# Expert outputs added in memory by accumulating DMAs, with the routing weights gathered beside the token rows

## The chip, the core and the metric

The kernel runs on one core of a Trainium2 chip. A core has a matrix engine (TensorE, PE in the profile; its weight loads are PEld), a vector engine (VectorE, DVE), a scalar engine (ScalarE, ACT), a general engine (GpSimd, POOL) and a sequencer that issues DMAs (SyncE, SP). Each engine takes its instructions in order, and they meet through semaphores. On-chip memory is SBUF (128 partitions) and PSUM (128 partitions, banks that matrix products are written to); inputs, outputs and scratch tensors are in HBM, reached by 16 DMA engines. Plain DMAs are issued here by SyncE. Indirect DMAs, which take a row number for each of 128 partitions, are issued by GpSimd.

The metric is the device time of one execution in microseconds (us). The kernel before took 928.88 us, the median of three runs (928.79 to 930.76).

## The reference, cut to what matters

Six layers work on x of 64 x 32 = 2048 tokens with 256 features; each adds its result to x. Two attention layers, an fp8 linear layer, a cross attention with a context of 257 keys and a gated low-rank mixer come first. The change is in the last layer, a mixture of experts on the normalized tokens:

```python
flat = hidden.reshape(T, d)                              # 2048 x 256
router_probs = softmax(flat @ router_w + router_b)       # 8 experts
topk_probs, topk_idx = top_k(router_probs, 2)
weights = zeros_like(router_probs).at[arange(T)[:, None], topk_idx].add(topk_probs)
sh = gelu(flat @ sw1 + sb1, approximate=False)           # the shared expert
shared_out = sh @ sw2 + sb2
h1 = gelu(einsum('td,edh->teh', flat, rw1) + rb1[None], approximate=False)
expert_out = einsum('teh,ehd->ted', h1, rw2) + rb2[None]
mixed = einsum('ted,te->td', expert_out, weights)
return shared_out + mixed                                # added to x
```

Each token needs only its two chosen experts. The hidden width is 512, and all of this is in float32.

## The kernel before

**Tokens.** x stays in SBUF as four groups `xs[g]` of 128 x 4 x 256: partition p of tile t in group g is token g*512 + t*128 + p. At the start of the last layer the normalized rows `y` are stored in the HBM tensor `y_rows` (2048 rows of 256 numbers) and, transposed, kept in SBUF for the router and the shared expert. The helper `normed` does this for some tiles of a group; `choose` turns router products into the probabilities `pe` and two one-hot choices `best`.

**Routing.** `mixture` sorts the 4096 pairs of token and expert into tiles that belong to one expert each. There are 16 places for wide tiles (256 rows, `n` = 2, numbers j = 0 to 15) and further narrow ones (128 rows, `n` = 1, j from 16 on). `MS` = 20 tiles are always computed, 16 wide and 4 narrow; up to 3 more are in a branch (`tc.If(count > MS)`), which these inputs do not take. VectorE works out the place of each pair (`pos`) and the probability of each choice (`pw`, by `picked`). Then it writes one-hot matrices `in_tile` and `at`, and TensorE multiplies them in four batches into `ps_inv`, which holds for each place of each tile the row number of its pair: 1 to 2048 for a first choice, 2049 to 4096 for a second one, 0 for none. From it come `read_i` (which row of `y_rows` to gather) and `write_i` (which row to write the result to; a spare row where the place is empty).

**The expert loop.** For tile j: `gather(j)` fetches rows of `y_rows` into `yg`, one indirect DMA for each 128 rows; `first_weights` and `second_weights` load w1, w2 and the bias b2 of the tile's expert (514, 512 and 128 KB); `by_feature` transposes the rows on TensorE (`ps_yg`); `hidden` computes `ps_h` on TensorE and gelu on ScalarE; `outputs` computes `ps_o` on TensorE, adds b2 on VectorE (`og`) and scatters the rows by one indirect DMA for each 128 rows into the HBM tensor `r_rows`, which has a row for each pair. The scatters are declared independent of one another. The loop is written out by hand: iteration j gathers tile j+3, transposes tile j+1, computes the hidden layer of j and the outputs of j-1. Buffers come from rings of three or four tiles.

**The shared expert.** Its hidden layer is computed in 16 pieces (`fill_hidden`), its output in 16 units (`fill_outputs`), one for each 128 tokens: four matrix products into half a PSUM bank, `ps_so`. After two units VectorE owes an addition of the full bank to x (`owed`, paid by `settle`). Seven units are placed by hand within the routing, three before the loop, six after it.

**The end.** After the last tile SyncE loads all of `r_rows` back (8 DMAs `r<-r_rows` of 512 KB), and `sum_up` adds to x the two expert rows of each token, each times its `pw`, in 32 VectorE instructions, and stores x to `out`.

Names in the profile: L106 is the line of a helper that issues nearly all instructions of VectorE, ScalarE, GpSimd and SyncE; L118 and L121 are matrix products and transposes. So groups are told apart by their tiles. A scheduler settles the final order of each engine's instructions, where the kernel does not ask for program order.

Of the kernel before, what the change touches and what calls it, by code (L numbers as in the profile page):

```python
# [7 lines left out]
F32 = mybir.dt.float32  # L8
# [56 lines left out]
def perceiver_kernel(ctx: ExitStack, tc: tile.TileContext, a: dict, out: bass.AP):  # L65
# [810 lines left out]
    def normed(g, ts, eng=None, by_act=True):  # L876

        n, t0 = len(ts), ts[0]
        x = xs[g]
        steps = norm_steps(g, eng, True, ts, by_act)  # L880
        next(steps)
        yield
        next(steps)
        yield
        if n > 2:
            next(steps)
            yield
        y = finish(steps)
        sync.dma_start(
            out=y_rows.rearrange("(g t p) d -> g p t d", g=NG, p=P)[g][:, t0 : t0 + n], in_=y  # L890
        )
# [58 lines left out]

    hid_bank, out_bank = either("b3", "b4"), ring(psum, "b2", "b6")
    hidden_rows = {}
# [13 lines left out]
    def shared_outputs(g, t):  # L966
        if t % 2 == 0:
            out_rows[0] = out_bank([P, 2, D], "ps_so")
# [12 lines left out]

    out_rows = [None]
    owed = []

    def settle():
# [11 lines left out]
    def fill_outputs(n):  # L997
        for _ in range(n):
            shared_outputs(*next(output_units))
# [482 lines left out]
    def mixture():  # L1482
        nt = nt_all
        n2 = 2 * nt

        r_rows = nc.dram_tensor("r_rows", (2 * NB * S + MH * P, D), F32, kind="Internal").ap()
        pm = ring(psum, "b5", "b7")
# [3 lines left out]
        def carved(tag, shape, name, dt=F32, size=256):  # L1491
# [13 lines left out]
            return part  # L1505

        rc = sb.tile([P, N_ROUTE], F32, tag="n0", name="rc")
        sync.dma_start(out=rc, in_=a["route"])
# [33 lines left out]
        fill_outputs(1)  # L1542
        next(last_norm)
        next(last_norm)
        next(early, None)
# [27 lines left out]
        fill_hidden(7)  # L1573
        pos, pw = carved("w8", [n2], "pos"), carved("w8", [n2], "pw")

        def picked(which, dst, src):
            pick = carved(("f4", "lx0")[which], [nt, NE], "pick")
            vector.tensor_tensor(pick, best[which], src, ALU.mult)
            vector.tensor_reduce(dst[:, which * nt : (which + 1) * nt], pick, AX.X, ALU.add)

        for which in range(2):
            picked(which, pw, pe)

# [46 lines left out]
        for which in range(2):  # L1630
            picked(which, pos, place)
        pos_i = carved("lx3", [n2], "pos_i", I32)
# [30 lines left out]
        b2_ = ring(sb, "lx0", "lx1", "lx2")  # L1663
        yg_, ygT_ = ring(sb, "n1", "p0", "p1", "sc0"), ring(sb, "sc1", "eT0")
        hTr_, og_ = ring(sb, "q0", "q1"), ring(sb, "e0", "e1", "e2", "eT1")

# [5 lines left out]
        def gather(j):  # L1672
            n, at = its[j]["n"], its[j]["at"]
            its[j]["yg"] = yg = yg_([P, n, D], "yg")
# [30 lines left out]

        for j in range(3):
            first_weights(j)
# [62 lines left out]
        write_i = carved("lv1", [MH], "write_i", I32)  # L1770
        vector.scalar_tensor_tensor(write_i, row1, -1.0, spare, ALU.add, ALU.add)

        def by_feature(it):
# [24 lines left out]

        written = []

        def outputs(it):
            n, hT, w2, b2 = it["n"], it["hT"], it["w2"], it["b2"]
            ps = po([P, n, D], "ps_o")
            for i in range(n):
                for c in range(4):
# [6 lines left out]
                    )  # L1812
            o = og_([P, n, D], "og")
            vector.tensor_tensor(o, ps, b2[:, None, :].to_broadcast([P, n, D]), ALU.add)
            for i in range(n):
                at = it["at"] + i
                wrote = nc.gpsimd.indirect_dma_start(  # L1817
                    out=r_rows,
                    out_offset=bass.IndirectOffsetOnAxis(ap=write_i[:, at : at + 1], axis=0),
                    in_=o[:, i, :],  # L1820
                    in_offset=None,
                )
                for earlier in written:
                    tc.declare_no_dep(wrote.ins, earlier, reason="no two places have one row")
                tc.keep_in_program_order(wrote)
                written.append(wrote.ins)

        for j in range(3):
            gather(j)
        for j in range(2):  # L1830
            second_weights(j)

        count = nc.values_load(
# [19 lines left out]
        settle()  # L1853
        by_feature(its[0])
        for j in range(MS):
            if j + 3 < MS:
                gather(j + 3)
            if j + 1 < MS:
                by_feature(its[j + 1])
            hidden(its[j])  # L1860
            if j + 3 < MS:
                first_weights(j + 3)
            if j > 0:
                outputs(its[j - 1])
            if j + 2 < MS:
                second_weights(j + 2)
        outputs(its[MS - 1])


        r_view = r_rows[: 2 * NB * S].rearrange("(w g t p) d -> g p w t d", w=2, g=NG, p=P)  # L1870
        whole = sb.tile([P, 4, NT, D], F32, tag="kb0", name="r")
        r = [(whole[:, 0], whole[:, 1]), (whole[:, 2], whole[:, 3])]
        r_ = ring(sb, *wide[0:4])
        r += [tuple(r_([P, NT, D], "r") for _ in range(2)) for _ in range(2)]
        for g in range(NG):
            for which in range(2):
                sync.dma_start(out=r[g][which], in_=r_view[g, :, which])

        def sum_up(g):
            for t in range(NT):  # L1880
                x = xs[g][:, t, :]
                for which in range(2):
                    at = which * nt + g * NT + t
                    vector.scalar_tensor_tensor(
                        x, r[g][which][:, t, :], pw[:, at : at + 1], x, ALU.mult, ALU.add
                    )
                if t % 2 == 1:
                    sync.dma_start(out=out_view[g][:, t - 1 : t + 1], in_=xs[g][:, t - 1 : t + 1])

        fill_outputs(4)  # L1890
        settle()
        sum_up(0)
        fill_outputs(2)
        settle()
        for g in range(1, NG):
            sum_up(g)

    out_view = out.rearrange("(g t p) d -> g p t d", g=NG, p=P)
    mixture()
# [33 lines left out]
def _routing():  # L1933
# [10 lines left out]
    c[:, T_COL : T_COL + MT] = [2 * j if j < MF else MF + j for j in range(MT)]  # L1944
    c[:, T_SPARE : T_SPARE + MH] = 2 * NB * S + 1 + np.arange(MH) * P + p[:, None]
    return c
# [107 lines left out]
```

## Time and profile before

| | us |
|---|---|
| median of three runs | 928.88 |
| the profiled execution | 928.56 |
| its span, first to last instruction | 926.8 |
| PE busy | 856.0 |
| PEld busy | 588.5 |
| DVE busy | 605.3 |
| POOL busy | 501.1 |
| ACT busy | 424.1 |
| start of the last layer's routing table load (rc) | 697.6 |
| first gather of expert rows | 759.2 |
| first ps_h of the expert loop | 768.0 |
| last og written | 900.3 |
| last store to out issued | 923.6 |

The busy times are shares of the whole span, of which the first 700 us are attention. The last layer is read from the instructions' order in time: up to 759 us the routing, to 768 the first gathers, to 900 the expert loop, then the end. The page also cuts the span into 40 slices of 23.2 us and prints the busy share of each in tenths (9 is 90% or more); the last nine digits of each row, from 718 us on, are the routing, the expert loop and the end. PEclk is the TensorE clock that was granted, in tenths of full speed; DMA is the mean busy share of the 16 DMA engines:

```profile
PE   6899999979899999999999999999889889999993
DVE  7888888897677677675777666878654872111116
PEclk9999999989999999999999999999799979999997
DMA  7445333543110111111110112000001046777758
```

### The profile page before, as it was taken

What the parts mean: (1) busy time and instruction counts of PE and PEld (TensorE: products, weight loads), DVE (VectorE), ACT (ScalarE), POOL (GpSimd) and SP (SyncE); (2) the same over time, 40 slices, a digit from 0 to 9 for tenths busy, and PEclk for the clock granted to TensorE, in tenths of its full rate; (3) what the DMA queues carried; (4) which work ended last, traced back from release to release, by engine and by line L of the source; (5) the groups of instructions that cost most, each with busy time, mean ns of one, the idle gap of its engine ahead of it and who ended that gap; (6) DMA issues with size and microseconds to landing.
All of it is one profiled execution on the core that took longest, in us unless ns stands there. A gap on an engine that the chain in (4) does not pass through costs nothing. (4 is left out here: it accounts for less than half of the span.)

```text
span 926.8 us, 22828 instructions
## 1 busy us (share of the span) xinstructions
PE 856.0 (92%) x8699; PEld 588.5 (63%) x8699; DVE 605.3 (65%) x1755; ACT 424.1 (46%) x1099; POOL 501.1 (54%) x982
## 2 busy tenths in 40 slices
PE   6899999979899999999999999999889889999993
PEld 3566666656456666666656666565656648888882
DVE  7888888897677677675777666878654872111116
ACT  2566666645555555554555456564443212222210
POOL 3567667764674656564664747656531214555430
PEclk9999999989999999999999999999799979999997
DMA  7445333543110111111110112000001046777758
GB/s 240 140 133 141 85 88 101 132 115 104 53 52 8 46 53 53 52 54 52 53 52 3 52 52 98 2 2 24 2 23 35 24 143 189 235 240 229 216 182 272
DMA packets 66926, 88.79 MB, mean 96 GB/s; under 512 B 32480, under 2 KB 50688, under 8 KB 64768
## 3 DMA queue, kind: packets, MB, share of 16 engines
q1 hardware_dynamic: 63264, 77.75, 27.6%
q0 software_dynamic: 3456, 9.44, 3.1%
q8 instruction: 69, 1.13, 0.5%
q14 instruction: 41, 0.34, 0.1%
q10 hardware_dynamic: 96, 0.13, 0.1%
HBM read 65.80 MB, written 13.11 MB: 85 GB/s over the span
## 5 line engine op out<-in xcount | busy, mean ns | idle before, releaser
L106 ACT ACTIVATE e<-e,xnm 128x257 f32<-128x257 f32 x256 | 127.2, 498 | 51.5 <-DVE xnm L106 45.5
L106 DVE CUSTOM_DVE_ANT_0 e<-ps_s,mask 128x257 f32<-128x257 f32 x256 | 93.5, 421 | 49.6 <-PE ps_s L118 47.9
L118 PE MATMUL ps_k<-ct,w_w_l1x 128*128 128x512 f32 x256 | 122.3, 600 | 1.6 <-ACT yT L106 0.6
L106 POOL TENSOR_SCALAR e<-e,xsm 128x256 f32<-128x256 f32 x256 | 121.8, 496 | 0.0
L118 PE MATMUL ps_v<-w_w_l1x,ct 128*128 128x256 f32 x512 | 121.8, 381 | 0.0
L121 PE MATMUL ps_t<-cst,e 128*128 128x128 f32 x640 | 102.9, 284 | 7.8 <-DVE eT L106 6.9
L106 DVE COPY eT<-ps_t 128x512 f32<-128x512 f32 x128 | 88.0, 687 | 30.3 <-PE ps_t L121 30.1
L118 PEld LDWEIGHTS ps_v<-w_w_l1x,ct 128*128 128x128 f32 x512 | 93.9, 191 | 11.0 <-issue 0.2
L106 POOL TENSOR_TENSOR x<-x,rows 128x256 f32<-128x256 f32 x96 | 71.3, 759 | 46.2 <-ACT y L106 19.4
L106 ACT ACTIVATE kT<-ps_k,vec 128x512 f32<-128x512 f32 x64 | 44.1, 689 | 100.5 <-PE ps_k L118 100.3
L121 PEld LDWEIGHTS ps_t<-cst,e 128*128 128x128 f32 x640 | 72.1, 142 | 26.4 <-DVE eT L106 7.8
L106 ACT ACTIVATE hTr<-ps_h,w 128x256 f32<-128x256 f32 (+1 forms) x80 | 31.4, 450 | 115.0 <-issue 82.7
L106 DVE TENSOR_TENSOR og<-ps_o,b 128x512 f32<-128x512 f32 (+1 forms) x20 | 12.8, 638 | 105.6 <-PE ps_o L118 105.6
L118 PEld LDWEIGHTS ps_k<-ct,w_w_l1x 128*128 128x128 f32 x256 | 44.5, 190 | 41.3 <-issue 35.3
L1817 POOL DMA_INDIRECT r_rows<-og,lv x36 | 35.6, 989 | 60.9 <-DVE og L106 56.0
L118 PE MATMUL ps_h<-ygT,w 128*128 128x256 f32 (+1 forms) x320 | 65.8, 359 | 0.6 <-issue 0.6
L118 PE MATMUL ps_o<-w,hTr 128*128 128x256 f32 x288 | 65.3, 379 | 0.0
L106 ACT COPY v<-ps_v 128x512 f32<-128x512 f32 x80 | 46.4, 582 | 39.5 <-PE ps_v L118 39.4
L106 POOL TENSOR_TENSOR last<-e,xsm 128x4 f32<-128x4 f32 x64 | 13.0, 204 | 88.4 <-DVE xsm L106 88.0
L118 PEld LDWEIGHTS ps_h<-ygT,w 128*128 128x128 f32 x320 | 54.9, 190 | 6.6 <-issue 0.8
L118 PEld LDWEIGHTS ps_o<-w,hTr 128*128 128x128 f32 x288 | 54.4, 190 | 7.2
L106 ACT ACTIVATE kb<-kT,cst 128x256 f32<-128x256 f32 x96 | 45.4, 512 | 26.7 <-POOL kT L106 25.1
(210 smaller groups left out, 1677.2 us busy)
## 6 DMA issues: line engine op xcount, KB each, us to landing
ct<-in_ctxT SPq DMA_DIRECT2D x16, 1024.0 KB, 5.4
w<-in_ew SPq DMA_DIRECT2D x20, 514.0 KB, 3.6
w<-in_ew SPq DMA_DIRECT2D x20, 512.0 KB, 3.7
far<-part SPq DMA_DIRECT2D x126, 64.0 KB, 2.3
v_rows<-v SPq DMA_DIRECT2D x16, 256.0 KB, 2.3
vb<-v_rows SPq DMA_DIRECT2D x64, 64.0 KB, 2.1
r<-r_rows SPq DMA_DIRECT2D x8, 512.0 KB, 8.2
b<-in_eb SPq DMA_DIRECT2D x20, 128.0 KB, 3.8
```

The costliest lines, as they stand in the source:

```text
L106: ins = getattr(self.engine, name)(*args, **kw)
L118: return kept(nc.tensor.matmul(ps, **args))
L121: return kept(nc.tensor.transpose(ps, src, eye))
L1817: wrote = nc.gpsimd.indirect_dma_start(out=r_rows, out_offset=bass.IndirectOffsetOnAxis(ap=write_i[:, at : at + 1], axis=0), in_=o[:, i, : ...
```

## The change

It touches the last layer alone.

- `y_rows` gets 258 columns. The two probabilities of each token (`pw`, now with the two choices side by side) are stored into the last two by one DMA, 16 x 128 pieces of 8 bytes, and come with the rows in each gather (`yg` has 258 columns).
- `by_feature` picks for each row the probability that belongs to the pair (`mine` tells first from second choice) into `it["share"]`, by two small VectorE instructions.
- `outputs` scales: for each 128 rows ScalarE writes `b2w` = b2 * share, and VectorE `og` = ps_o * share + b2w.
- The scatter goes into `out` itself and adds there (`compute_op=ALU.add`). Only the scatters of one tile are declared independent of each other; between tiles the dependency on `out` stays. Empty places write to 256 spare rows behind the 2048 of `out`, which are cut off on the host and filled once from a constant tile.
- x with the shared expert's output is stored to `out` as soon as each pair of units is added (`stored`). All 16 units of the shared output stand before the loop: eight in the first part of the routing, two before the ps_inv batches, one between the second and the third batch, two before the branch and three after it. They use five PSUM banks in a new order.
- The tiles are taken in the order `line`: 0, 16, 1, 2, 17, 3, 4, 18, 5, 6, 19, 7, ... 15, so that narrow tiles stand between wide ones.
- `r_rows`, its loads, the 32 additions and the stores behind them are gone.

```diff
-    y_rows = nc.dram_tensor("y_rows", (NB * S, D), F32, kind="Internal").ap()
+    y_rows = nc.dram_tensor("y_rows", (NB * S, D + 2), F32, kind="Internal").ap()
...
-            owed.append(lambda: vector.tensor_tensor(x, ps, x, ALU.add))
+
+            def stored():
+                vector.tensor_tensor(x, ps, x, ALU.add)
+                sync.dma_start(out=out_view[g][:, t - 1 : t + 1], in_=x)
+
+            owed.append(stored)
...
+        out_banks[0] = ring(psum, "b2", "b6", "b2", "b6", "b1", "b2", "b0", "b6")
...
         next(last_norm)
+        fill_outputs(1)
         next(last_norm)
...
         for which in range(2):
-            picked(which, pw, pe)
+            picked(which, pw[:, :, which], pe)
+        sync.dma_start(
+            out=y_rows.rearrange("(t p) d -> p t d", p=P)[:, :, D : D + 2], in_=pw
+        )
...
-        for j in range(3):
+        line = [0, 16, 1, 2, 17, 3, 4, 18, 5, 6, 19, *range(7, MF)]
+        for j in line[:3]:
             first_weights(j)
...
+        fill_outputs(2)
         for i in range(0, n2, per):
+            if i == 2 * per:
+                fill_outputs(1)
...
+            share = small.tile([P, n, 2], F32, tag="share", name="share")
+            vector.tensor_tensor(
+                share, it["yg"][:, :, D : D + 2], mine[:, it["at"] : it["at"] + n], ALU.mult
+            )
+            it["share"] = small.tile([P, n], F32, tag="shares", name="shares")
+            vector.tensor_reduce(it["share"], share, AX.X, ALU.add)
...
-            vector.tensor_tensor(o, ps, b2[:, None, :].to_broadcast([P, n, D]), ALU.add)
+            for i in range(n):
+                share = it["share"][:, i : i + 1]
+                b2w = b2w_([P, D], "b2w")
+                scalar.activation(b2w, b2, AF.Copy, scale=share)
+                vector.scalar_tensor_tensor(
+                    o[:, i, :], ps[:, i, :], share, b2w, ALU.mult, ALU.add
+                )
             for i in range(n):
                 at = it["at"] + i
-                wrote = nc.gpsimd.indirect_dma_start(
-                    out=r_rows,
+                ins = nc.gpsimd.indirect_dma_start(
+                    out=out,
                     out_offset=bass.IndirectOffsetOnAxis(ap=write_i[:, at : at + 1], axis=0),
                     in_=o[:, i, :],
                     in_offset=None,
+                    compute_op=ALU.add,
                 )
-                for earlier in written:
+                for earlier in wrote:
...
+        fill_outputs(2)
+        settle()
...
-        for j in range(MS):
-            if j + 3 < MS:
-                gather(j + 3)
+        for at in range(MS):
+            if at + 3 < MS:
+                gather(line[at + 3])
...
-        for g in range(NG):
-            for which in range(2):
-                sync.dma_start(out=r[g][which], in_=r_view[g, :, which])
-
-        def sum_up(g):
-            for t in range(NT):
-                x = xs[g][:, t, :]
-                for which in range(2):
-                    at = which * nt + g * NT + t
-                    vector.scalar_tensor_tensor(
-                        x, r[g][which][:, t, :], pw[:, at : at + 1], x, ALU.mult, ALU.add
-                    )
```

More of the change, by code (lines that the diff above doesn't have):

```diff
@@ L848, in perceiver_kernel @@
     nt_all = NG * NT
-    y_rows = nc.dram_tensor("y_rows", (NB * S, D), F32, kind="Internal").ap()
+    y_rows = nc.dram_tensor("y_rows", (NB * S, D + 2), F32, kind="Internal").ap()
+    y_view = y_rows.rearrange("(g t p) d -> g p t d", g=NG, p=P)
     yTs, route = {}, {}
@@ L888, in normed @@
         y = finish(steps)
-        sync.dma_start(
-            out=y_rows.rearrange("(g t p) d -> g p t d", g=NG, p=P)[g][:, t0 : t0 + n], in_=y
-        )
+        sync.dma_start(out=y_view[g][:, t0 : t0 + n, 0:D], in_=y)
         for t in ts:
@@ L948, in choose @@
         vector.tensor_tensor(part("chosen", "c0", [NE], BF16), *best, ALU.add)
-    hid_bank, out_bank = either("b3", "b4"), ring(psum, "b2", "b6")
+    hid_bank, out_banks = either("b3", "b4"), [ring(psum, "b2", "b6")]
     hidden_rows = {}
@@ L967, in shared_outputs @@
         if t % 2 == 0:
-            out_rows[0] = out_bank([P, 2, D], "ps_so")
+            out_rows[0] = out_banks[0]([P, 2, D], "ps_so")
         ps = out_rows[0]
@@ L979, in shared_outputs @@
             x = xs[g][:, t - 1 : t + 1, :]
-            owed.append(lambda: vector.tensor_tensor(x, ps, x, ALU.add))
+            def stored():
+                vector.tensor_tensor(x, ps, x, ALU.add)
+                sync.dma_start(out=out_view[g][:, t - 1 : t + 1], in_=x)
+            owed.append(stored)
     out_rows = [None]
     owed = []
+    out_view = out[: NB * S].rearrange("(g t p) d -> g p t d", g=NG, p=P)
     def settle():
@@ L1484, in mixture @@
         n2 = 2 * nt
-        r_rows = nc.dram_tensor("r_rows", (2 * NB * S + MH * P, D), F32, kind="Internal").ap()
         pm = ring(psum, "b5", "b7")
@@ L1505, in carved @@
             return part
+        for i in range(2):
+            sync.dma_start(
+                out=out[NB * S + i * P : NB * S + (i + 1) * P], in_=rows[:, 0:D]
+            )
+        out_banks[0] = ring(psum, "b2", "b6", "b2", "b6", "b1", "b2", "b0", "b6")
         rc = sb.tile([P, N_ROUTE], F32, tag="n0", name="rc")
@@ L1573, in mixture @@
         fill_hidden(7)
-        pos, pw = carved("w8", [n2], "pos"), carved("w8", [n2], "pw")
+        pos, pw = carved("w8", [n2], "pos"), carved("w8", [nt, 2], "pw")
         def picked(which, dst, src):
@@ L1578, in picked @@
             vector.tensor_tensor(pick, best[which], src, ALU.mult)
-            vector.tensor_reduce(dst[:, which * nt : (which + 1) * nt], pick, AX.X, ALU.add)
+            vector.tensor_reduce(dst, pick, AX.X, ALU.add)
         for which in range(2):
-            picked(which, pw, pe)
+            picked(which, pw[:, :, which], pe)
+        sync.dma_start(
+            out=y_rows.rearrange("(t p) d -> p t d", p=P)[:, :, D : D + 2], in_=pw
+        )
         t_i = carved("w8", [2, NE], "t_i", I32)
@@ L1630, in mixture @@
         for which in range(2):
-            picked(which, pos, place)
+            picked(which, pos[:, which * nt : (which + 1) * nt], place)
         pos_i = carved("lx3", [n2], "pos_i", I32)
@@ L1664, in mixture @@
         yg_, ygT_ = ring(sb, "n1", "p0", "p1", "sc0"), ring(sb, "sc1", "eT0")
+        b2w_ = ring(sb, "r0", "r1", "r2")
         hTr_, og_ = ring(sb, "q0", "q1"), ring(sb, "e0", "e1", "e2", "eT1")
@@ L1673, in gather @@
             n, at = its[j]["n"], its[j]["at"]
-            its[j]["yg"] = yg = yg_([P, n, D], "yg")
+            its[j]["yg"] = yg = yg_([P, n, D + 2], "yg")
             for i in range(n):
@@ L1770, in mixture @@
         write_i = carved("lv1", [MH], "write_i", I32)
-        vector.scalar_tensor_tensor(write_i, row1, -1.0, spare, ALU.add, ALU.add)
+        vector.tensor_tensor(write_i, spare, read_i, ALU.add)
+        mine = carved("lv1", [MH, 2], "mine")
+        vector.tensor_scalar(mine[:, :, 0], row1, float(NB * S), None, ALU.is_le)
+        vector.tensor_scalar(mine[:, :, 1], row1, float(NB * S), None, ALU.is_gt)
         def by_feature(it):
@@ L1797, in hidden @@
                     )
-        written = []
         def outputs(it):
@@ L1803, in outputs @@
             ps = po([P, n, D], "ps_o")
+            o = og_([P, n, D], "og")
+            wrote = []
             for i in range(n):
@@ L1812, in outputs @@
                     )
[L1813 to L1814 removed]
+            for i in range(n):
[4 more added lines that the diff above has]
+                    o[:, i, :], ps[:, i, :], share, b2w, ALU.mult, ALU.add
+                )
             for i in range(n):
                 at = it["at"] + i
[L1817 to L1818 removed]
+                ins = nc.gpsimd.indirect_dma_start(
+                    out=out,
                     out_offset=bass.IndirectOffsetOnAxis(ap=write_i[:, at : at + 1], axis=0),
@@ L1821, in outputs @@
                     in_offset=None,
+                    compute_op=ALU.add,
                 )
-                for earlier in written:
[L1824 to L1828, printed above, removed]
+                for earlier in wrote:
+                    tc.declare_no_dep(
+                        ins.ins, earlier, reason="an expert has a token once, spare rows are not read"
+                    )
+                tc.keep_in_program_order(ins)
+                wrote.append(ins.ins)
+        for j in line[:3]:
             gather(j)
-        for j in range(2):
+        for j in line[:2]:
             second_weights(j)
+        fill_outputs(2)
+        settle()
         count = nc.values_load(
@@ L1853, in mixture @@
         settle()
-        by_feature(its[0])
-        for j in range(MS):
-            if j + 3 < MS:
-                gather(j + 3)
[L1858 to L1874, printed above, removed]
-        for g in range(NG):
-            for which in range(2):
-                sync.dma_start(out=r[g][which], in_=r_view[g, :, which])
-        def sum_up(g):
-            for t in range(NT):
-                x = xs[g][:, t, :]
-                for which in range(2):
-                    at = which * nt + g * NT + t
-                    vector.scalar_tensor_tensor(
-                        x, r[g][which][:, t, :], pw[:, at : at + 1], x, ALU.mult, ALU.add
[L1886 to L1898, printed above, removed]
+        by_feature(its[line[0]])
+        for at in range(MS):
+            if at + 3 < MS:
+                gather(line[at + 3])
+            if at + 1 < MS:
+                by_feature(its[line[at + 1]])
+            hidden(its[line[at]])
+            if at + 3 < MS:
+                first_weights(line[at + 3])
+            if at > 0:
+                outputs(its[line[at - 1]])
+            if at + 2 < MS:
+                second_weights(line[at + 2])
+        outputs(its[line[-1]])
     mixture()
@@ L1944, in _routing @@
     c[:, T_COL : T_COL + MT] = [2 * j if j < MF else MF + j for j in range(MT)]
-    c[:, T_SPARE : T_SPARE + MH] = 2 * NB * S + 1 + np.arange(MH) * P + p[:, None]
+    c[:, T_SPARE : T_SPARE + MH] = NB * S + np.arange(MH) % 2 * P + p[:, None]
     return c
@@ L2048 @@
         args[name] = nc.dram_tensor(f"in_{name}", m.shape, mybir.dt.from_np(m.dtype), kind="ExternalInput").ap()
-    out = nc.dram_tensor("out", (NB * S, D), F32, kind="ExternalOutput").ap()
+    out = nc.dram_tensor("out", (NB * S + 2 * P, D), F32, kind="ExternalOutput").ap()
     with tile.TileContext(nc) as tc:
@@ L2052 @@
     r = run_bass_kernel_spmd(nc, [arrays], core_ids=[0])
-    return r.results[0]["out"].reshape(NB, S, D)
+    return r.results[0]["out"][: NB * S].reshape(NB, S, D)
```

## The prediction

> **What bounds the kernel now.** I read the end first, the last steps of the chain of waits, in order of time (start us, us, what):
>
> ```profile
> 896.38 3.47 PE ps_o L118 x16
> 899.88 0.43 DVE og L106
> ```
>
> Before these two lines the chain is TensorE alone from 768.01 us on: a wide tile costs 0.44 (ps_yg) + 3.46 (ps_h) + 3.45 (ps_o) = 7.35 us. So TensorE sets the time of the expert loop, and the last product ends at 896.38 + 3.47 = 899.85. What comes after it is in the timeline of the last 27 us (start, duration, engine, instruction, idle before):
>
> ```profile
> 900.36 10.63 PE L118 MATMUL ps_so<-w_shared,hT 128*128 128x256 f32 x48 [0.52 <-DVE og L106]
> 900.58 0.97 POOL L1817 DMA_INDIRECT r_rows<-og,lv  x1 [0.75 <-DVE og L106]
> 903.14 7.19 SPq L106 DMA_DIRECT2D r<-r_rows  x8
> ...
> 910.42 13.56 SPq L106 DMA_DIRECT2D out<-x  x8
> 911.91 0.68 DVE L106 TENSOR_TENSOR x<-ps_so,x 128x512 f32<-128x512 f32 x1
> 912.51 11.08 DVE L106 SCALAR_TENSOR_TENSOR x<-r,w,x 128x256 f32<-128x256 f32 x24
> ```
>
> Six shared output units are left for the end, all expert rows are read back after the last scatter, and VectorE adds them in 32 instructions. From 899.85 to the span's end at 926.8 pass 26.95 us without an expert product. Last, the table of stretches around the routing (stretch, length, PE, PEld, DVE, ACT, POOL busy, granted TensorE clock, DMA share, GB/s):
>
> ```profile
> 750.00:753.00 3.00, 0.94 (x10) 0.34 (x8) 3.00 (x3) 0.69 (x1) 0.00 (x0) 1.00 1.03 409
> 753.00:756.00 3.00, 1.46 (x21) 1.16 (x22) 2.85 (x5) 0.00 (x0) 0.00 (x0) 0.74 1.02 400
> 756.00:759.00 3.00, 2.94 (x13) 2.34 (x11) 1.67 (x7) 0.00 (x0) 0.00 (x0) 0.50 0.26 90
> 759.00:762.00 3.00, 2.07 (x5) 1.20 (x5) 0.69 (x1) 0.00 (x0) 2.20 (x3) 0.50 0.16 44
> ...
> 775.00:850.00 75.00, 75.00 (x369) 66.06 (x368) 12.89 (x20) 17.64 (x42) 38.47 (x39) 1.00 0.73 236
> ```
>
> TensorE idles while VectorE sorts tokens to tiles, and then its clock falls to 0.50. In the loop it is busy all the time, GpSimd about half of it, and the DMA engines 0.73.
>
> **Removed.** The whole end: 6 units, 8 loads of 512 KB, 32 additions, 8 stores. Minus 26.95 us.
>
> **Moved: the six units.** One unit is 8 matmul records at 0.216 us, 1.73 us (two of them are the 3.45 of ps_o); six are 10.4 us. I follow them through the timeline of the routing and the changed program's order of instructions.
>
> ```profile
> 732.75 0.68 DVE L106 TENSOR_TENSOR x<-ps_so,x 128x512 f32<-128x512 f32 x1
> 733.35 0.17 DVE L106 TENSOR_TENSOR lg<-ps_r,rows 128x16 f32<-128x16 f32 x1
> ...
> 756.47 3.75 PE L118 MATMUL ps_so<-w_shared,hT 128*128 128x256 f32 x8
> ...
> 759.20 1.20 POOL L106 DMA_INDIRECT yg<-y_rows,lv  x1 [29.10 <-DVE lv L106]
> ```
>
> One unit goes in before the last normalization's transposes. That puts the unit that begins the fourth pair in front of the last router product; it needs the bank that the addition at 732.75 frees at 733.43. So it runs 733.5 to 735.2, the router product (0.95) ends at 736.15, and lg is written at 736.2 and not 733.35: +2.85 us for all that follows, 1.73 of it work and the rest a new wait.
>
> Two units stand before the sorting products ps_inv and one between their second and third batch. The hidden products end at 750.47 + 2.85 = 753.3, the two units at 756.8, two batches of 0.47, a unit, two batches: 760.4. Without the units it would be 756.41 + 2.85 = 759.3. From ps_inv to the first gather took 759.20 - 756.44 = 2.76; one addition of 0.69 inside it now stands later, two small new instructions (0.2 each, as their neighbours of 39 columns) may stand before it: first gather at 762.5 to 763.2, the second 1.5 later, landed after 3.2: 767.9 at the latest. TensorE meanwhile does three units (5.2, to 765.6), the branch (0.93 idle now), two units (3.45): ps_yg at 770.0 and not 766.42. **+3.6 us**; the gathers stay hidden with 2 us to spare. That six units cost so little has two covers: idle of 1.83 + 0.67 + 0.67 + 0.43 us before the ps_inv batches, and the half clock, which makes the unit at 756.47 last 3.75 and two more 5.43 us, 4.0 above full speed. If the clock still falls there, add about 4 us; if the bank wait is no wait, take 1 to 2 off. I keep 1.5 to 8.
>
> The row for the clock is 0.50 at 756 to 762, after 2.1 us idle in three. The Trainium skill (TensorE: Matmul & The Clock Gate, Part 1: The HAM clock gate) explains it as a gate that halves the clock after an idle window of about 3.4 us; the trace has no idle that long, only sparse use. By the page's letter no idle of 3.4 us means no loss at all in either kernel; by the row the fill is worth 4 us, and the row decides.
>
> **Added in the loop.** TensorE's work is the same 131.84 us (768.01 to 899.85), in another order of tiles. VectorE: per wide tile two additions with a scale (0.48 each, as conv with a PSUM source) for one of 0.69, and two tiny ones of 0.2: +0.7 on 1.4 of 7.35 us. ScalarE: two scaled copies of 0.51 (as kb) behind four of 0.47. GpSimd: as many DMAs as now. SyncE: the new 8-byte stores of the weights (2048 pieces) stand in front of the expert weights, at 741 on idle queues, 20 us before the first gather; the nearest row, 256 pieces in 2.1 us, makes 2 to 17 us of them. All hidden by TensorE; without cover the VectorE part would be 20 x 0.7 = 14 us. The stores of x, now on SyncE ahead of the fourth tile's weights, wait for the last addition at about 771, before the first ps_h (771.6 + 3.46) frees that buffer anyway. Rows of 1032 bytes instead of 1024: nothing.
>
> **Added: a chain.** Now no scatter waits for another one; the 60.9 us idle before them is og:
>
> ```profile
> L1817 POOL DMA_INDIRECT r_rows<-og,lv x36 | 35.6, 989 | 60.9 <-DVE og L106 56.0
> ```
>
> In the changed program the scatters add to one tensor, and each tile's first one waits until the tile before has landed. Behind it on GpSimd stand its partner and the gathers of three tiles ahead, on which TensorE waits only if the delay passes some 14 us (three tiles at 132/20 = 6.6, less 2.5 to issue and 3.2 to land). The trace has no accumulating DMA. Its landing L is bounded by these (KB are not given; us from issue to landing):
>
> ```profile
> yg<-y_rows,lv POOLq DMA_INDIRECT x36, 3.2
> r_rows<-og,lv POOLq DMA_INDIRECT x36, 3.2
> ```
>
> At least the plain scatter, 3.2; at most a gather and a scatter one after the other, 6.4. Nearer to the scatter, because issue (0.99) and completion are paid once: I take 4.4. The chain over 20 tiles is 20 x (L + 0.1) + 16 x 1.3 for the partners = 22.8 + 20 L, from about 779.6; with 4.4 that is 110.8 us, under TensorE's. So only the end counts. The second-to-last tile's second scatter issues 3.45 - 0.8 = 2.65 us before the last product's end (0.8 is 899.85 to 900.58, with 0.48 for 0.42); the last tile's follow at -2.55 + L and 1.3 later, and land at -1.25 + 2 L = 7.55 after the product. From the last landing to the span's end I take 0.8, as now (store at 923.6, landed 2.4 later, end 926.8). **+8.35 us**; 5.95 with L = 3.2.
>
> The Trainium skill (DMA: Bandwidth & Descriptors, Rules for kernel authors) speaks against the change: an accumulate reads its destination first and writes it later, so another access must wait for its semaphore. The program does wait, so by the rule the chain above is the least there is; no run here shows what fails without it.
>
> **Sum.** 926.8 - 26.95 + 3.6 + 8.35 = 911.8 us span. The profiled execution took 928.56, so 1.76 lie around the span: 913.6. Its time is 0.3 under the median of the three runs, 928.88, which I leave aside.
>
> **Rivals.**
> *The chain of accumulates becomes the bound.* Its end is 779.6 + 22.8 + 20 L, against 902.15 + 2 L from TensorE: it decides from L = 5.5, and with the 0.8 and 1.76 the kernel is slower than 928.56 from L = 6.2. At 6.4, the upper bound, 933; at 8 it would be 965. For it: 20 us per us of L, and bounds that reach it. Against it: reading and adding 1 KB should not cost a second full DMA. 13%.
> *Half of it is given back*, by L between 5.5 and 6.2 or by full DMA engines. Scatters move 36 x 128 KB in 131.8 us, 36 of the 236 GB/s, or 0.11 of the share 0.73; at 3.5 times their price the engines are full. With L = 5.9: 923. 9%.
> *Everything is hidden*: front 1.5, L = 3.2: 926.8 - 26.95 + 1.5 + 5.95 + 1.76 = 909. For it: the covers counted above. Against it: the bank wait is in the order of instructions. 13%.
> *The forecast*, 65%, with its own range 909.5 to 919: front 1.5 to 8 and L up to 5.
>
> **Numbers.** 913.6 is the likeliest. 907 to 926 leaves out the slower case and a little on both sides. Under 0.2% (1.9 us) a change can't be told from none. Faster: 65 + 13 + nearly all of 9 = 0.85; slower 0.12; the same 0.03.
>
> **What would show it.** Right: ps_yg of the first tile near 770, granted clock near 1.00 from 750 to 768, last ps_o near 903.4 with no idle in the loop, two scatters after it and the end 8 us later. Landing of the accumulating scatters near 4.4. Wrong: og or the gathers waiting for scatters in the loop, a DMA share near 1.00, the 8-byte stores landing after 762, or TensorE idle before ps_so at 733 longer than 1.5 us.

## The result, and the profile after

| | before | after | predicted |
|---|---|---|---|
| median of 17 runs each, us | 929.46 | 935.4 | 913.6 |
| ratio, 95% interval | | 1.0059 (1.0048 to 1.0071) | |
| span of the profiled execution | 926.8 | 932.9 | 911.8 |
| first ps_h of the loop | 768.0 | 772.5 | 771.6 |
| end of the last ps_o | 899.85 | 918.7 | 903.4 |
| from there to the span's end | 26.95 | 14.2 | 8.35 |

The kernel is 0.6% slower. The spans can be split at the first ps_h and at the last ps_o: the front grew by 4.5 us, the loop by 14.4 (131.8 to 146.2), and the end shrank by 12.7. The prediction had +3.6, 0 and -18.6. So the loop took more than the end gave, and of the loop the forecast said that nothing changes there. Of the front's 4.5 us, 1.2 lie before the changed part: the last transposes into ps_t, ahead of the routing, are that much later already (from 600 to 700 us, kernel before, then after: count, duration ns min/median/max, first and last start us).

```profile
L121 PE MATMUL ps_t<-cst,e x88: 272/273/476, 605.3 to 695.6; 128*128 128x128 f32 x88
...
L121 PE MATMUL ps_t<-cst,e x92: 272/273/476, 601.1 to 696.9; 128*128 128x128 f32 x92
```

The change's own front is therefore 3.3 us; in the runs below with plain scatters, without the chain and with earlier gathers the first ps_h comes at 771.3 to 771.7.

First the slices that were shown of before, now of the kernel after (slices of 23.3 us, the last nine digits from 723 us on):

```profile
PE   6899999979899999999999999998989899889993
DVE  7888888897677677675777666878745772212210
PEclk9999999989999999999999999999899999999997
DMA  7555333443110111111110113000001257987873
```

The 7 in PEclk, the half clock in the routing, is gone. In the loop the PE row has two 8s where before it was 9 throughout, and the DMA row, 7s before, goes up to 9. TensorE's waits between 772 and 920 us (engine, line, what it waited for: total us, times, longest) and the groups of GpSimd in the same stretch say who holds it up:

```profile
PE ps_yg L121 <- DMA yg<-y_rows,lv: 7.6, 6, 1.9
...
L1850 POOL DMA_INDIRECT out<-og,lv x36 | 57.2, 1588 | 58.3 <-DMA out<-og,lv 21.7 <-issue 18.7 <-DVE og L106 14.9
```

The scatter's issue occupies GpSimd for 1.59 us; the plain one took 0.99. Of its idle time before scatters, 21.7 us now end with the landing of another scatter, which never happened before, and 14.9 with `og`, where it was 56. The chain of waits shows how this reaches TensorE (start us, us, what; "DMA x" is the time from the start of the issue to the landing):

```profile
772.53 3.69 PE ps_h L118 x16
...
782.78 1.63 POOL out L1850
...
814.16 6.01 DMA out<-og,lv
...
820.25 0.75 issue
821.00 1.63 POOL out L1850
...
822.93 5.66 DMA out<-og,lv
...
831.64 1.56 POOL out L1850
...
833.51 1.02 POOL yg L106
...
834.84 5.04 DMA yg<-y_rows,lv
839.92 0.55 PE ps_yg L121 x3
...
885.06 5.14 PE ps_h L118 x16
```

The first two rows are the first ps_h of the loop and the first scatter. Later a scatter lands 6.01 us after its issue; GpSimd needs 0.75 more before the next one starts; that one's partner starts 1.9 later and lands after 5.66. The gathers of a later tile stand behind all this, and TensorE waits for them at 839.9. After such a pause its clock is lower: the ps_h at 885.06 takes 5.14 us and not 3.46. Three stretches of 3.4 us have half the clock (PE busy, granted clock, DMA share, GB/s), after waits for gathers of 2.3, 2.6 and 1.9 us; after the one short wait of 0.8, at 801, the clock stays.

```profile
817.20:820.60 3.40, 3.40 (x18) 0.50 0.75 203
841.10:844.50 3.40, 3.40 (x15) 0.50 0.38 104
885.40:888.80 3.40, 3.40 (x10) 0.51 0.94 173
```

In the table of stretches (PE, PEld, DVE, ACT, POOL busy, granted clock, DMA share, GB/s) two of the loop and two of the routing:

```profile
800.00:825.00 25.00, 21.86 (x107) 19.00 (x106) 5.39 (x16) 6.47 (x17) 14.39 (x12) 0.93 0.80 210
850.00:875.00 25.00, 25.00 (x123) 21.84 (x121) 4.71 (x14) 9.04 (x23) 14.74 (x12) 1.00 0.86 239
```

```profile
750.00:756.00 6.00, 6.00 (x18) 3.21 (x18) 5.86 (x8) 2.34 (x4) 0.00 (x0) 1.00 0.50 172
756.00:762.00 6.00, 6.00 (x56) 5.25 (x55) 4.79 (x11) 0.00 (x0) 0.00 (x0) 1.00 0.83 313
```

The routing's TensorE is filled and its clock stays at 1.00, where before it was 0.50 from 756 to 762: this part came as forecast. Last the end, in the timeline (start, duration, engine, instruction, idle before):

```profile
911.64 7.07 PE L118 MATMUL ps_o<-w,hTr 128*128 128x256 f32 x32
...
916.26 1.55 POOL L1850 DMA_INDIRECT out<-og,lv  x1 [3.11 <-DVE og L106]
918.11 1.55 POOL L1850 DMA_INDIRECT out<-og,lv  x1 [0.30 <-issue]
918.80 0.88 DVE L106 SCALAR_TENSOR_TENSOR og<-ps_o,shares,b2w 128x256 f32<-128x256 f32 x2 [2.58 <-issue]
922.64 1.55 POOL L1850 DMA_INDIRECT out<-og,lv  x1 [2.97 <-DMA out<-og,lv]
924.50 1.55 POOL L1850 DMA_INDIRECT out<-og,lv  x1 [0.30 <-issue]
```

The last `og` is done at 919.7, but its scatter starts at 922.64: the one at 918.11 landed at 921.86 and GpSimd took 0.78 to go on. From these rows one step of the chain is L + 0.78 for a narrow tile (L is a scatter's time from the start of its issue to its landing) and 1.85 more for a wide one (first scatter to partner; up to 1.94 in the loop). The first scatters of the first and the last tile start at 782.78 and 922.64, 19 steps apart: 7.36 us each, against TensorE's 131.84 / 20 = 6.59. In four of these steps (those before 814.16, 836.85, 850.95 and 896.78, 7.1 us each) GpSimd was issuing gathers until 1.0 to 1.1 us before the scatter, so there its own queue was about as late as the landing, and the trace doesn't tell which of the two decided.

### The profile page after: what moved, and what is told of

It reads as the page before. It is cut to its first block, busy times and chain, and to the rows that moved or that the text cites. A ratio compares the mean times of both kernels' runs of the same rounds, so it can differ in the third digit from the quotient of the medians.

```text
span 932.9 us, 22903 instructions
## 1 busy us (share of the span) xinstructions
PE 856.3 (92%) x8699; PEld 588.9 (63%) x8699; DVE 600.6 (64%) x1781; ACT 438.2 (47%) x1135; POOL 521.0 (56%) x982
## 3 DMA queue, kind: packets, MB, share of 16 engines
q0 software_dynamic: 6912, 9.48, 5.8%
## 5 line engine op out<-in xcount | busy, mean ns | idle before, releaser
L1850 POOL DMA_INDIRECT out<-og,lv x36 | 57.2, 1588 | 58.3 <-DMA out<-og,lv 21.7
L106 DVE SCALAR_TENSOR_TENSOR og<-ps_o,shares,b2w 128x256 f32<-128x256 f32 x36 | 16.0, 480 | 105.0 <-PE ps_o L118 90.4
L118 PE MATMUL ps_h<-ygT,w 128*128 128x256 f32 (+1 forms) x320 | 70.0, 376 | 0.8 <-issue 0.8
L118 PEld LDWEIGHTS ps_h<-ygT,w 128*128 128x128 f32 x320 | 58.5, 204 | 7.4 <-issue 1.1
L106 POOL DMA_INDIRECT yg<-y_rows,lv x36 | 35.6, 989 | 43.7 <-PE ps_so L118 31.6
```

Of the source, the lines that this page charges most:

```text
L106: ins = getattr(self.engine, name)(*args, **kw)
L118: return kept(nc.tensor.matmul(ps, **args))
L1850: ins = nc.gpsimd.indirect_dma_start(out=out, out_offset=bass.IndirectOffsetOnAxis(ap=write_i[:, at : at + 1], axis=0), in_=o[:, i, :], in ...
```

## The experiments

The theory: one step of the chain, and nothing else, is on average longer than TensorE's tile. Rivals: the waits alone would have done it with plain scatters too; the accumulating DMAs fill the DMA engines or GpSimd, with or without waits; the gathers stuck behind the scatters are the cause and not a sign; the order of tiles; the moved units. All ratios are to the kernel before, run beside it on the same chip.

**Plain scatters, all waits kept.**

```diff
-                    compute_op=ALU.add,
```

> The changed kernel with plain scatters into out instead of adding ones; every wait between tiles stays. The additions are left out: a row of out keeps what was written last. Theory A (the wait for the tile before is dear because an adding scatter issues in 1.6 us and lands 4 to 6.5 us after its issue, and gathers stand behind it): with 1.0 us and about 3.2 us the chain fits under TensorE, the loop from first ps_h to last ps_o falls from 146 to about 132 us, and the kernel takes 913 to 918. Rival B (any wait between tiles costs this, whatever it waits for): the loop stays above 140 and the time above 928.

Measured: 917.67 us, ratio 0.9877 (0.9858 to 0.9895). GpSimd's waits, then the group on the page, of this kernel:

```profile
POOL out L1850 <- DMA out<-og,lv: 2.2, 1, 2.2
...
L1850 POOL DMA_INDIRECT out<-og,lv x36 | 35.6, 989 | 62.5 <-DVE og L106 50.1
```

One wait of 2.2 us for a landing, in the last tile, is left. The loop is 132 us. The same waits cost nothing with a DMA that is issued in 0.99 us and lands 3.9 us after the start of its issue (median): a wide step is then about 1.3 + 3.9 + 0.78 = 6.0. All else that the change adds to the loop (two scaled additions, scaled bias, the 258-column rows) is in this kernel too and is hidden, as predicted.

**Accumulating scatters without the chain.** Each pair adds into a row of its own in a tensor that is filled long before (71 tiles of 128 rows, written in the attention part), so no scatter waits for another tile's.

```diff
-            wrote = []
...
-                    out=out,
+                    out=r_rows,
```

> Adding scatters as in the changed kernel, but each pair has its own row in a scratch tensor filled beforehand in the attention part, so no scatter waits for another tile's. The last sum over a token's two rows is left out. Theory A (the waits): no idle before ps_yg in the loop, 132 to 134 us of loop, 913 to 918 us in all, landing times as in the changed kernel. Rival C (the adding DMAs themselves are too dear, by GpSimd's 1.6 us of issue or by the DMA engines' time): GpSimd or the DMA engines stay full, the loop stays near 140 or more, above 926 in all.

Measured: 918.75 us, 0.9892 (0.9872 to 0.9911). A group and two stretches:

```profile
L1858 POOL DMA_INDIRECT r_rows<-og,lv x36 | 57.2, 1589 | 41.8 <-DVE og L106 35.4
...
800.00:825.00 25.00, 25.00 (x131) 22.17 (x131) 6.41 (x22) 8.55 (x22) 18.27 (x15) 1.00 1.00 264
825.00:850.00 25.00, 24.57 (x130) 21.63 (x129) 5.12 (x15) 8.95 (x23) 17.33 (x14) 1.00 0.98 272
```

The accumulate's whole price is here: 1.59 us to issue, landing 5.1 (3.8 to 6.5), DMA share up to 1.00. TensorE stays at 25.00 of 25 and 24.57. So neither the DMAs nor the waits are too much by themselves; the two together are.

**Two chains.** Tiles at odd positions of the order add into a second tensor, so each waits for the tile two before it.

```diff
+            targets.append(r_rows if len(targets) % 2 else out)
...
-                    out=out,
+                    out=targets[-1],
```

> The changed kernel with two targets: tiles at odd positions of the order add into a second tensor (filled early), so that each tile waits for the tile two before it; the sum of the two tensors is left out. If the bound is one step of the chain (issue 1.55 or 3.1, landing 5, wake 0.7, together 7.3 us against 6.6 of TensorE), two steps now have 13.2 us: the waits vanish, the loop is 132 us again, the last products end at 904 to 905, the span is 914 to 917, the time 916 to 920. If several accumulates under way at once lengthen each other (two chains run side by side), landings pass 8 us and the time stays above 925.

Measured: 919.39 us, 0.9881 (0.9852 to 0.9909). TensorE's waits from 770 to 910 are

```profile
PE ps_h L118 <- issue: 0.8, 1, 0.8
PE ps_yg L121 <- DMA yg<-y_rows,lv: 0.3, 1, 0.3
```

and the landing has a median of 4.9. Accumulates that run side by side don't lengthen each other past the step; with 13.2 us for it the bound is gone.

**Gathers further ahead.** Six tiles instead of three, with eight buffers.

```diff
-        for j in line[:3]:
+        for j in line[:6]:
             gather(j)
...
-            if at + 3 < MS:
-                gather(line[at + 3])
+            if at + 6 < MS:
+                gather(line[at + 6])
```

> The changed kernel with gathers issued six tiles ahead instead of three, into eight buffers. Theory A1 (TensorE loses time only because gathers stand in GpSimd's queue behind waiting scatters): TensorE no longer waits for gathers, the loop falls to 133 to 136, 916 to 921 in all. Theory A2 (the chain of scatters itself is as long as the loop: about 7.4 us between first scatters of tiles): the gathers come in time, but the last scatter still starts at about 920 and the time stays within 928 to 936, with og waiting for its buffers.

Measured: 936.54 us, 1.0080 (1.0053 to 1.0106), no faster than the changed kernel (the profiled execution, 930.76, was the fastest of five). A stretch of the loop, then the end:

```profile
825.00:850.00 25.00, 25.00 (x133) 22.22 (x133) 5.59 (x17) 8.94 (x23) 15.27 (x12) 1.00 0.94 268
...
903.55 0.88 DVE L106 SCALAR_TENSOR_TENSOR og<-ps_o,shares,b2w 128x256 f32<-128x256 f32 x2 [2.58 <-issue]
905.93 1.55 POOL L1851 DMA_INDIRECT out<-og,lv  x1 [3.05 <-DMA out<-og,lv]
...
918.76 1.55 POOL L1851 DMA_INDIRECT out<-og,lv  x1 [2.99 <-DMA out<-og,lv]
920.62 1.55 POOL L1851 DMA_INDIRECT out<-og,lv  x1 [0.30 <-issue]
```

TensorE is whole again: last product at 903.5, loop 132 us, clock 1.00. But the scatters don't follow: with all of `og` ready at 904.4, three tiles are still to be added, the last at 918.76. The stuck gathers were only how TensorE felt the chain. This run separates the two most plainly.

**No weight loads.** The weights of the first three tiles are used again for all others.

```diff
             if at + 3 < MS:
-                first_weights(line[at + 3])
+                its[line[at + 3]]["w1"] = its[line[at]]["w1"]
...
-            if at + 2 < MS:
-                second_weights(line[at + 2])
+            if at == 0:
+                second_weights(line[2])
+            elif at + 2 < MS:
+                for key in ("w2", "b2"):
+                    its[line[at + 2]][key] = its[line[at - 1]][key]
```

> The changed kernel with expert weights loaded for the first three tiles only and reused by the others, so later tiles use wrong weights; loads of 17 tiles are left out. If the adding scatters land late because they share the DMA engines with 1.15 MB of weights per tile: landing falls to the 3.7 us after issue seen at the end of the changed kernel, the tiles come every 6.6 us, the loop is 132 to 134 and the time 915 to 919. If the landing time is the adding DMA's own: it stays at 5 to 6.5 us and the time above 926.

Measured: 921.36 us, 0.9925 (0.9900 to 0.9950); all times of a scatter together, then a stretch:

```profile
DMA to landing us min/median/max: 3.6/3.8/4.7
...
825.00:850.00 25.00, 25.00 (x131) 22.17 (x130) 5.24 (x17) 8.95 (x23) 19.14 (x16) 1.00 0.49 84
```

Alone, an accumulating scatter lands in 3.8 us; beside the weight loads it takes 5. With 3.8 a step is on average 3.8 + 0.78 + 0.8 x 1.85 = 6.06, under 6.59, and the chain again costs only 3.0 us of waits at the last tile. The loop is 132 us, as expected; the time is above the 915 to 919 expected, since the end still takes 14.0 us (11.0 with plain scatters).

**The order of tiles.** The changed kernel with the tiles in the order 0 to 19.

```diff
-        line = [0, 16, 1, 2, 17, 3, 4, 18, 5, 6, 19, *range(7, MF)]
+        line = [*range(MS)]
```

> The changed kernel with its tiles in natural order, the four narrow ones last. Chain theory: a narrow tile takes TensorE 3.74 us but the chain about 6, so four in a row leave the scatters behind: the end lies up to 4 x 2.3 = 9 us later there, while the wide tiles at 7.35 just cover their 7.4 us of chain, so the loop before them is freer by 5 to 10 us; in all 930 to 940. If the order is what costs the changed kernel its time (loads and gathers of narrow tiles early): 920 to 926.

Measured: 934.06 us (924.6 to 938.0), 1.0020 (0.9987 to 1.0054). The spread is too wide to say that the order matters. It is not what makes the kernel slow: the loop of the profiled execution still takes 144.6 us, with 34.8 of GpSimd's waits before scatters ended by landings.

**Parts of the change by themselves.** First the 16 shared units before the loop, in the kernel before, with the changed kernel's places and banks:

```diff
+        fill_outputs(2)
         for i in range(0, n2, per):
+            if i == 2 * per:
+                fill_outputs(1)
...
-        fill_outputs(4)
-        settle()
         sum_up(0)
-        fill_outputs(2)
-        settle()
```

> The kernel before with one part of the change alone: all sixteen shared units before the loop, in the changed kernel's places. Expert rows still go to the scratch tensor and are summed at the end. From the changed kernel's trace (first ps_h at 772.5 and not 768.0) the front costs 4.5 us. If the six units at the end were hidden under the loads of the rows, nothing comes back: 932 to 934. If they held VectorE's sums up by their three additions of 0.69 us and the last pair's end at 911.9, 2 to 4 us come back: 929 to 932.

Measured: 932.26 us, 1.0024 (1.0011 to 1.0037). First ps_h at 772.84, 4.8 later, of which 1.5 lie before the changed part (last ps_t at 697.1), so that the move costs 3.3 as in the changed kernel; the end shrinks from 26.95 only to 26.3. The six units there were hidden by the loads of `r_rows`: VectorE now waits 7.9 us for these. So moving them is a loss unless the loads go too.

Then the weights with the rows, in the kernel before: scaled outputs, plain scatters into `r_rows`, and at the end 16 additions of 512 columns instead of 32 of 256 with a scale.

```diff
-            for t in range(NT):
-                x = xs[g][:, t, :]
+            for t in range(0, NT, 2):
+                x = xs[g][:, t : t + 2, :]
                 for which in range(2):
-                    at = which * nt + g * NT + t
-                    vector.scalar_tensor_tensor(
-                        x, r[g][which][:, t, :], pw[:, at : at + 1], x, ALU.mult, ALU.add
-                    )
+                    vector.tensor_tensor(x, r[g][which][:, t : t + 2, :], x, ALU.add)
```

> The kernel before with another part alone: weights gathered with the rows and applied in the loop, plain scatters into the scratch tensor. The end then only adds: 16 additions of 512 columns in place of 32 scaled ones of 256. If the added VectorE and ScalarE work in the loop is hidden, the loop stays at 132; the end's VectorE time falls from 32 x 0.48 = 15.4 to 16 x about 0.65 = 10.4 us, bounded by the loads of 4 MB (about 11 us from 903): 921 to 925. If the loop's added work or the wider gathered rows cost, the loop is longer and the gain is lost: 928 or more.

Measured: 927.01 us, 0.9964 (0.9951 to 0.9978): faster than both kernels, but above the 921 to 925 expected (the kernel before took 930.29 beside it). VectorE's additions at the end, first of the kernel before, then of this one (count, then busy us and mean ns):

```profile
L106 DVE SCALAR_TENSOR_TENSOR x<-r,w,x 128x256 f32<-128x256 f32 x32 | 14.3, 482 | 0.6
...
L106 DVE TENSOR_TENSOR x<-r,x 128x512 f32<-128x512 f32 x16 | 10.5, 688 | 0.6 <-DVE x L106 0.4
```

The additions take 10.5 us instead of 14.3 and end at 920.5 instead of 923.6; the loop is unchanged.

Last, the same with four of these additions, those of the second group, on GpSimd, and this group's sums first and its stores later:

```diff
-                    vector.tensor_tensor(x, r[g][which][:, t : t + 2, :], x, ALU.add)
+                    (gpsimd if g == 1 else vector).tensor_tensor(
+                        x, r[g][which][:, t : t + 2, :], x, ALU.add
+                    )
```

> The kernel before with weights gathered with the rows (as e4_scaled), and the four final additions of the second group on GpSimd (1.3 us each, beside VectorE). If VectorE's 16 additions (0.68 each) bound the end, its last one ends 2.7 us earlier, at 917.8, and the time is 923.5 to 925 (ratio 0.994 to 0.996). If the loads and stores of r and out bound it (4 MB in 12 us, 2 MB behind them), it stays at 926 to 927.

Measured: 928.4 us, 0.9979 (0.9966 to 0.9993), no better than without and above both times expected. The same group shows why:

```profile
L106 DVE TENSOR_TENSOR x<-r,x 128x512 f32<-128x512 f32 x12 | 11.0, 941 | 0.8 <-DMA r<-r_rows 0.6
```

Twelve additions take as long as sixteen did: 0.94 us on average. Nine take the 0.68 or 0.69 of before; the three that take 1.63 to 1.75 each start while one of GpSimd's additions (1.3 to 1.6 us) is running. The Trainium skill (SBUF — State Buffer, Who interferes with whom) has the rule: a VectorE instruction with two SBUF inputs and a GpSimd instruction that reads SBUF share a read interface, and one waits for the whole of the other. These three agree with it.

**The end of the program.** The kernel before, with its very last store issued by GpSimd.

```diff
-                    sync.dma_start(out=out_view[g][:, t - 1 : t + 1], in_=xs[g][:, t - 1 : t + 1])
+                    (gpsimd if g == NG - 1 and t == NT - 1 else sync).dma_start(
+                        out=out_view[g][:, t - 1 : t + 1], in_=xs[g][:, t - 1 : t + 1]
+                    )
```

> The kernel before with its very last store issued by GpSimd in place of SyncE; nothing else. Theory: after the last landing of a GpSimd DMA the program needs some 4 to 5 us to end, against 0.8 after one of SyncE: the span grows by 1 for the issue and some 4 more, to 930 to 932, the time to 932 to 934. Rival: the end costs the same from every queue, and the 4.6 us after the last accumulating scatter are a landing longer than the record shows: span 927 to 928.5, time 929 to 930.5.

Measured: 935.17 us, 1.0056 (1.0036 to 1.0077), span 931.3:

```profile
923.61 0.79 POOL L106 DMA_DIRECT2D out<-x  x1 [22.34 <-DVE x L106]
...
out<-x POOLq DMA_DIRECT2D x1, 256.0 KB, 2.6
```

The store starts at the same 923.6 as SyncE's did and lands at 926.2; the program ends 5.1 us after that, where before it ended 0.8 after the landing (with the median landing of 2.4). What runs in that time is an instruction named `DRAIN`, which GpSimd executes on the kernel's last line, the first and longest of three. Its rows in the kernel before, in the changed one, in the run with four additions on GpSimd and in this one (count, duration ns min/median/max, first and last start us):

```profile
L2050 POOLq DRAIN  x3: 45/113/7166, 900.3 to 926.5; - x3
L2058 POOLq DRAIN  x3: 46/113/9137, 922.9 to 932.6; - x3
L2074 POOLq DRAIN  x3: 45/113/7609, 915.3 to 924.8; - x3
L2052 POOLq DRAIN  x3: 40/118/6866, 923.6 to 931.0; - x3
```

They end at 907.5, 932.0, 922.9 and 930.5, each 6.0 us (5.96 to 6.05) after GpSimd's last instruction has ended: a scatter's issue at 901.55 and 926.05, an addition at 916.88, the store's issue at 924.40. So it is neither the queue nor the landing of the last DMA that costs the 4 us, but that GpSimd works to the end. In the changed kernel and in this one the program ends 0.85 after the `DRAIN`; in the kernel before and in the run with the additions it is hidden under VectorE's sums and the stores.

## Why the prediction was wrong

**The step that failed** is the chain: "per tile L + 0.1, 1.3 per partner", 22.8 + 20 L, with L = 4.4, "under TensorE's. So only the end counts". The mechanism was in the text, as the first rival with 13%, and its place and its effect were as described there; gathers waiting for scatters in the loop were named as a sign of being wrong, and came. What was off are three terms of one step, mean over 16 wide and 4 narrow tiles (the page of the changed kernel has no landing times; 5.1 is the median of the run without the chain and of the one in natural order):

| term | predicted | measured | more, per tile |
|---|---|---|---|
| landing L | 4.4 | 5.1 beside weight loads (3.8 alone) | 0.7 |
| from landing to the next issue | 0.1 | 0.78 | 0.68 |
| first scatter to its partner, wide tiles only | 1.3 | 1.85 | 0.44 |
| step | 5.54 | 7.36 | 1.82 |

The sum of the measured terms, 5.1 + 0.78 + 0.8 x 1.85 = 7.36, is just the step seen in the trace. (Besides, the chain begins at 782.78, 10.25 us after the first ps_h, where the 779.6 of the prediction is 8.0 after its 771.6: another 2.2 us, once.) Some 60% of the miss is in the two terms that the prediction did not bound: the partner's issue was taken as a plain scatter's, and from landing to issue 0.1 was taken without a row for it. No scatter of the kernel before waited for a landing, so its rows don't have this time: the 0.8 that was used for the end runs from the last product and has `og` in it, and from the end of `og` to the scatter it was 0.28. After a landing it is 0.78.

With those two as measured, the chain decides from L = 6.59 - 0.78 - 1.48 = 4.3, and not from the 5.5 that the rival was given: the chosen 4.4 was already on the other side. The bounds of L (3.2 to 6.4) held for the median; single landings took up to 6.5. The argument "reading and adding 1 KB should not cost a second full DMA" held for the landing: 5.1 against the plain scatter's 3.9 in the same order, and 0.6 of the difference is the longer issue. It did not hold for the time of the DMA engines, which was not what decided. The queue of the indirect DMAs went from 3456 to 6912 packets: 36 scatters with 96 more each, 144 where a transfer had 48. Its share went from 3.1% to 5.8% of 16 engines' span; the difference, about 406 engine-us, is 11.3 per scatter on top of the 6.4 that the 72 plain transfers average: 2.8 times the price.

The Trainium skill (Collectives: The Full Stack, The bandwidth ceiling: the fold count and why AG ≠ RS ≠ AR) says of the addition in a ReduceScatter that it needs two source reads, and gives 1.93 for the bandwidth of AllGather over that of ReduceScatter. Taken over to a scatter, as an estimate, it is below the 2.8 in engine time here.

**The end, 14.2 and not 8.35.** Up to the last landing 9.55 us (taking 3.75 for the last scatter as for the one before it), 2.0 more than -1.25 + 2 L with L = 4.4. The second-to-last tile's second scatter was issued 0.6 us before the end of the last product and not 2.65, which is 2.05; the wake-up adds 0.68 and the partner 0.55; two landings of 3.75 take off 1.3. From there to the end about 4.6 instead of 0.8. That term was read from a kernel in which GpSimd had long been done; here the end is set by its `DRAIN`, 6.0 us after the last scatter's issue, and not by the landing.

**The front, 4.5 and not 3.6.** Without the 1.2 us that this execution was late before the changed part, it is 3.3, and the steps were right: idle at the branch 0.91 (0.93 predicted), clock 1.00. The first gather at 762.95 lies in the stated 762.5 to 763.2, and ps_yg at 770.87 is 0.9 later than summed, both with the 1.2 in them. The idle before the ps_so at 734.8, 1.63, was a little over the 1.5 that had been named as a sign of being wrong, without harm. Alone, in the kernel before, the move cost the same 3.3.

**The end's removal, -26.95,** was right as a whole, and so were the covers: VectorE, ScalarE, the wider rows and the weights' store cost nothing in the run with plain scatters. "Half of it is given back by full DMA engines" fell: a share of 1.00 left the loop as it was.

**The size.** 21.1 us between 911.8 and 932.9: 0.9 up to the first ps_h (1.2 before the changed part, -0.3 in the front), 14.4 loop, 5.8 end. In the loop 7.6 are TensorE waiting for rows; 5.1 are the three stretches of 3.4 us at half the clock; the last 1.7 were not followed. All of it vanishes where the gathers run further ahead, and then the end takes them.

What stays open: why the plain scatter's landing was 3.9 in the changed order against 3.2 before, and why a scatter that waited for a landing starts 0.78 us after it while one that waited for `og` starts 0.28 after that.

## What to carry to other kernels

Before a chain of dependent DMAs is called hidden, write down one whole step (issue of every DMA in it, landing beside the loads that really run, wake-up of the engine that waits) and compare it with the time of one tile, not only the sum with the whole loop: here 7.36 stood against 6.59. Adding in memory saves the reading back but makes writers that were independent wait for one another; independent targets keep the stream free. What they cost in turn, one sum at the end, was left out in the runs here and is not measured. Parts of a change can be worth more than the whole: scaling within the loop alone gave 0.4%.

## What the runs showed of the hardware that was not expected

- An indirect DMA of 128 rows of 1 KB that adds takes GpSimd 1.59 us to issue (plain 0.99), three times the packets and some 2.8 times the engine time; it lands in 3.8 us on quiet DMA engines and 5.1 beside weight loads.
- From a DMA's landing to the start of the scatter that waited for it GpSimd took 0.78 us; from the end of `og` it was 0.28.
- GpSimd's `DRAIN` on the last line ended 6.0 us after GpSimd's last instruction in four kernels, after a scatter, a store and an addition alike. Where GpSimd was the last to work, the program ended 0.85 later, so that this is in the time: 5.1 us from the landing of a store, about 4.6 from that of a scatter.
- Waits of TensorE of 1.9 to 2.6 us, in one or two pieces, were followed by 3.4 us at half the clock; a single one of 0.8 was not.
- Of VectorE's additions from SBUF (0.69 us), those that began during one of GpSimd's took 1.63 to 1.75.
- A DMA share of 0.98 to 1.00 over 50 us left TensorE's loop at 132.7 us, against 131.8 before.
